# One layer's x + layernorm(x): from an addition on GpSimd to a second activation on ScalarE

## The chip, the core and the metric

The kernel runs on one core of a Trainium2 chip. A core has five engines that work side by side and meet at semaphores: TensorE (PE, matmuls and their weight loads), VectorE (DVE), ScalarE (ACT), GpSimd (POOL, which also starts transfers from its own queue) and SyncE (SP, which only starts transfers). The metric is the device time of one execution in microseconds; the time before is the median of three runs, 3288.75 us (3285.65 to 3289.74).

## The reference, cut to what matters

Four layers over x of 4 batches, 1024 rows, 256 columns, all float32:

```
x = x + attention_a(layernorm(x))    # 16 heads of 64
x = x + ffn(layernorm(x))            # 256 -> 1024, gelu, -> 256
x = x + attention_b(layernorm(x))    # layer 3: its function takes h = layernorm(x)
x = x + ffn(layernorm(x))
```

Attention b is called with h = layernorm(x). It normalizes h again (with a scale and a bias), projects down to two 128-wide codes, up to queries, keys and values, rotates queries and keys, and returns out + h: its own residual is the normalized input. So layer 3 is x + h + (the projected attention). The first two terms, x + layernorm(x), are what this case is about. With mean m and r = 1/sqrt(var + eps), layernorm(x) is x * r + (-m * r), and the sum is x * (1 + r) + (-m * r).

## The kernel before, in words

All of x stays on chip, one tile per batch (`xs[b]`, 128 partitions x 8 row tiles x 256 columns), and is updated in place by every layer. The order of work on each engine is written out by hand: the kernel runs under a manual schedule, and each engine executes its instructions in the order in which the Python code issues them.

An attention layer is a sequence of 256 steps: 4 batches x 8 pairs of heads x 8 query tiles of 128 rows (`steps_with`, from line 330). In a step TensorE makes the scores of the next query tile (`scores`, L238) into one of three score buffers for each of the two heads; VectorE takes the negated row maximum (L249); ScalarE makes the exponentials with their row sums (`exponentials`, L251); VectorE inverts the sums (L259), ScalarE spreads them over columns beside the exponentials (`invert`, L260), and VectorE transposes blocks of 32 x 32 into the tile T (`turn`, L271). Every second step, transfers rearrange T into pT: the last five of each group start from GpSimd's queue, the others from SP's (`send`, L295). TensorE multiplies pT by the values (`weigh`, L304) five steps behind; ScalarE copies the sums out (L314) and, in the second attention, copies one block of T to pT itself (`keep`, L287); GpSimd multiplies by the inverted row sums (`take`, L316); TensorE projects (`project`, L167), ScalarE copies the result out (L326) and GpSimd adds it to x (L328).

Work for the following pair and batch is hung into the steps through a table of pieces: the function `batch_b` gives each of its pieces a step number, and `steps_with` runs them after the exponentials or at the end of that step. The projections of the next pair (L647, L668 on ScalarE), the exchange of neighbouring rows (L652, transfers from GpSimd's queue) and the rotation (L657 to L659, three GpSimd operations) are such pieces. The weights of a pair come over SP's queue (L636, L212, L214).

`batch_b` prepares a batch for attention b in two blocks of four row tiles (qb = 0 and 1, t = 0 to 3). Its piece `first` makes layernorm(x) of one row tile into x1 with a ScalarE activation (`standardize`, L147) and lets GpSimd add it to x (L604). `second`, two steps later, scales x1 in place on ScalarE for the second normalization (L608), and `turned` transposes it on TensorE and copies it out (L153, L158). Batches 1 to 3 are prepared within the steps of the batch before them, one tile per step; batch 0 is prepared within the feed-forward layer ahead, where `rest` takes one or two pieces of this prologue behind each GELU (L414) of the last blocks.

The factors of a normalization are measured and finished by `scaling`: statistics (L126, L127) on VectorE, a square root on ScalarE (L130), and the reciprocal and products on VectorE (L131 to L138). In layer 3 it runs three times, over 8, 16 and 8 row tiles.

In the feed-forward layer (`ffn`) a block of 512 rows is standardized on ScalarE (L147, four activations in a row) with GpSimd adding the second bias to x (L396), transposed on TensorE and copied out by ScalarE (L156), multiplied into three buffers in turn (L410), passed through the GELU (L414), multiplied back (L421) and added to x on VectorE (L428).

Of the kernel before, what the change touches and what calls it, by code (L numbers as in the profile page):

```python
# [9 lines left out]
F32 = mybir.dt.float32  # L10
# [5 lines left out]
P = 128  # L16
# [7 lines left out]
NQB = S // QB  # L24
# [15 lines left out]
def hybrid_block_kernel(  # L40
# [5 lines left out]
    nc = tc.nc  # L46
# [3 lines left out]
    const = ctx.enter_context(tc.tile_pool(name="const", bufs=1))  # L50
# [8 lines left out]
    def group(*shape):  # L59
        last[0] ^= 1  # L60
        return ps_mm.tile([P, *shape], F32, tag=f"m{last[0]}", name="mm")
# [45 lines left out]
    def scaling(name, blocks, again=False):  # L107

        where = {}
        for b, qb in blocks:
            for t in range(TQ):
                where[b, qb * TQ + t] = len(where)
        m = len(where)
        mv = const.tile([P, m, 2], F32, name=f"{name}_mv")
        rstd = const.tile([P, m], F32, name=f"{name}_rstd")  # L120
        shift = const.tile([P, m], F32, name=f"{name}_shift")
        more = const.tile([P, m], F32, name=f"{name}_more") if again else None

        def measure(b, t):
            stats = small.tile([P, 6], F32, tag="stats", name="stats")
            nc.vector.bn_stats(stats, xs[b][:, t, :])  # L126
            nc.vector.bn_aggr(mv[:, where[b, t], :], stats)  # L127

        def finish():
            nc.scalar.activation(rstd, mv[:, :, 1], AF.Sqrt, bias=eps)  # L130
            nc.vector.reciprocal(rstd, rstd)  # L131
            if again:
                nc.vector.tensor_mul(more, mv[:, :, 1], rstd)
                nc.vector.tensor_mul(more, more, rstd)
                nc.scalar.activation(more, more, AF.Sqrt, bias=eps)
                nc.vector.reciprocal(more, more)
            nc.vector.tensor_mul(shift, mv[:, :, 0], rstd)
            nc.vector.tensor_scalar_mul(shift, shift, -1.0)  # L138

        def get(b, t):  # L140
            i = slice(where[b, t], where[b, t] + 1)
            return shift[:, i], rstd[:, i], more[:, i] if again else None

        return measure, finish, {k: (lambda k=k: get(*k)) for k in where}

    def standardize(dst, src, shift, rstd):
        nc.scalar.activation(dst, src, AF.Identity, scale=rstd, bias=shift)  # L147

    def transposed(dst, src, c, affine=None):

        tr = group(TQ, P)
        for t in range(TQ):
            nc.tensor.transpose(tr[:, t, :], src[:, t, ts(c, P)], ident)  # L153
        trf = tr.rearrange("p t q -> p (t q)")
        if affine is None:
            nc.scalar.copy(dst[:, c, :], trf)  # L156
        else:
            nc.scalar.activation(  # L158
                dst[:, c, :], trf, AF.Identity,
                scale=affine[0][:, c : c + 1], bias=affine[1][:, c : c + 1],  # L160
            )

    def paired(out, parts, first=True, last=True):

        for i, (lhsT, rhs) in enumerate(parts):
            for j in range(2):
                nc.tensor.matmul(  # L167
                    out[ts(j, DH)], lhsT[:, ts(j, DH)], rhs[j],
                    start=(first and i == 0), stop=(last and i == len(parts) - 1),
                )  # L170
# [413 lines left out]
    def layer_b(rows):  # L584

        scale_b = 1.0 / 8.0
        cs = {}

        def batch_b(b):
            work = []  # L590
            for qb in range(NQB):
                k = {}

                def first(t, b=b, k=k, qb=qb):
                    if t == 0:
                        if b:
                            k["x1"] = xnp.tile([P, TQ, D], F32, tag="xn", name="x1")
                        else:
                            k["x1"] = ptp.tile([P, SENT], F32, tag="pT", name="x1")[
                                :, : TQ * D  # L600
                            ].rearrange("p (t d) -> p t d", t=TQ)
                    xt = xs[b][:, qb * TQ + t, :]
                    standardize(k["x1"][:, t, :], xt, *rows.factors(NQB * b + qb, t)[:2])
                    nc.gpsimd.tensor_add(xt, xt, k["x1"][:, t, :])  # L604

                def second(t, b=b, k=k, qb=qb):
                    x1 = k["x1"][:, t, :]
                    nc.scalar.mul(x1, x1, rows.factors(NQB * b + qb, t)[2])  # L608

                def turned(c, b=b, k=k, qb=qb):  # L610
                    if c == 0:
                        p, tag = (highp, f"high{qb}") if b % 2 == 0 else (lowp, "low")
                        cs[b, qb] = p.tile([P, NC, QB], F32, tag=tag, name="hc")
                    transposed(cs[b, qb], k["x1"], c, affine=(lns_sb, lnb_sb))

                def down(m, b=b, qb=qb):

                    h = cs[b, qb][:, :, ts(m, QB // 2)]
                    pc = group(2, QB // 2)
                    for i in range(2):  # L620
                        paired(pc[:, i], [(wd_sb[:, i, c, :], [h[:, c]] * 2) for c in range(NC)])
                    nc.scalar.copy(h, pc)

                work += [(16 * qb - 14 + t, lambda t=t, f=first: f(t)) for t in range(TQ)]
                work += [(16 * qb - 12 + t, lambda t=t, f=second: f(t)) for t in range(TQ)]
                work += [(16 * qb - 8 + 2 * c - EARLY, lambda c=c, f=turned: f(c)) for c in range(NC)]
                work += [(16 * qb + 2 * m, lambda m=m, f=down: f(m)) for m in range(2)]
            return work

        def pair_b(b, pr):  # L630
            made, turned = {}, {}

            def load():
                w = made["w"] = wp.tile([P, 3, NC, P], F32, tag="w", name="w")[:, :, 0, :]
                for i, up in enumerate((wuq, wuk, wuv)):
                    nc.sync.dma_start(w[:, i], up[:, ts(pr, P)])  # L636

            def qk(i, qb):

                pq = group(QB)  # L640
                paired(pq, [(made["w"][:, i, :], [cs[b, qb][:, i]] * 2)])
                name = ("qT", "kT")[i]
                if qb == 0:
                    made[name] = qkp.tile([P, S], F32, tag=name, name=name)
                straight = made[name][:, ts(qb, QB)]
                made[i, qb] = straight
                nc.scalar.mul(straight, pq, (scale_b, 1.0)[i])  # L647

            def change(i, qb):
                turned[i, qb] = rp.tile([P, QB], F32, tag="turned", name="turned")  # L650
                for r in range(2):
                    nc.gpsimd.dma_start(turned[i, qb][r::2], made[i, qb][1 - r :: 2])  # L652

            def rotate(i, qb):

                straight, other = made[i, qb], turned.pop((i, qb))
                nc.gpsimd.tensor_mul(straight, straight, cos_sb[:, ts(qb, QB)])  # L657
                nc.gpsimd.tensor_mul(other, other, sin_sb[:, ts(qb, QB)])
                nc.gpsimd.tensor_add(straight, straight, other)  # L659

            def values(qb):
                if qb == 0:
                    made["v"] = vp.tile([P, NK2, DH], F32, tag="v", name="v")
                pv = group(NK2 // NQB, DH)
                for t in range(NK2 // NQB):
                    lhsT = cs[b, qb][:, 1, ts(t, DH)]
                    by_head(pv[:, t, :], [(lhsT, made["w"][:, 2, :])])
                nc.scalar.copy(made["v"][:, ts(qb, NK2 // NQB), :], pv)  # L668

            work = []  # L670
            for i in (1, 0):
                for qb in range(NQB):
                    k = 2 - 4 * i + 2 * qb
                    work += [(k - EARLY, lambda i=i, qb=qb: qk(i, qb))]
                    work += [(k + 1, lambda i=i, qb=qb: change(i, qb))]
                    work += [(k + 2, lambda i=i, qb=qb: rotate(i, qb))]
            work += [(4 + 2 * qb - EARLY, lambda qb=qb: values(qb)) for qb in range(NQB)]
            return {name: lambda name=name: made[name] for name in ("qT", "kT", "v")}, load, work

        return attention(batch_b, pair_b, wo_b, nc.sync, lead=5, kept=1)  # L680
# [8 lines left out]
    end_b, rest_b, _ = ffn_between(Rows("g", sets), True, n_steps)  # L689
# [66 lines left out]
```

## Time and profile before

| | before |
|---|---|
| median of three runs | 3288.75 us (3285.65, 3288.75, 3289.74) |
| profiled execution | 3283.29 us, its span 3281.4 us |
| mean granted TensorE clock | 0.996 |
| first attention, feed-forward, second attention, feed-forward | to about 1421, 1676, 3023, 3281 us of the span |
| GpSimd's additions L604 | 32, 734 ns (median), from 1562.9 to 2572.7 us |
| ScalarE's activations L147 of layer 3 | 32, 597 ns (median), from 1562.1 to 2571.1 us |

The profile is a record of one execution. It gives for every engine its busy time, for groups of equal instructions their count, their mean duration and what ended the idle time before them, and it follows the chain of waits back from the last instruction. L-numbers are lines of the kernel before. A timeline row has the start, the duration, the engine, the line, the operation, output and inputs, the count of instructions merged into the row, and in brackets the idle time before it with what released it. A row of a chain has the start, the time, the engine, what it worked on and the line. In a row of stretches the columns are the stretch and its length, then busy time and instruction count of TensorE, its weight loads, VectorE, ScalarE and GpSimd, the granted clock, the busy share of the DMA engines and what they moved in GB/s. The ends of matmuls are modelled, so that the end of one can lie a little past the start of the next.

### The profile page before, as it was taken

How to read it: one execution, taken by the hardware profiler on the slowest of the kernel's cores; microseconds unless marked ns; L12 is line 12 of the kernel's file. 1: busy time of each engine (PE TensorE's matmuls, PEld its weight loads, DVE VectorE, ACT ScalarE, POOL GpSimd, SP SyncE). 2: the span in 40 equal slices, each digit the busy share in tenths (PEclk: the TensorE clock that was granted, in tenths of full speed). 3: DMA queues.
4: the chain of work that ended last, by engine and by line, in shares of the span. 5: the costliest groups of instructions: out<-in, count | busy, mean ns of one | idle time of the engine just before them, and what ended most of it. 6: DMA issues, size and time to landing. Idle time of an engine off the chain costs nothing.

```text
span 3281.4 us, 126564 instructions
## 1 busy us (share of the span) xinstructions
PE 3201.6 (98%) x52736; PEld 2022.3 (62%) x52736; DVE 2531.3 (77%) x2386; ACT 2109.0 (64%) x4304; POOL 1958.4 (60%) x2738
## 2 busy tenths in 40 slices
PE   8999999999999999999999999999999999998999
PEld 4666666666666666666555556666656666665666
DVE  7988888888888888941049889998989999998100
ACT  5666666666666666642447777777778777777332
POOL 4544454545444445430159888998989999996110
PEclk9999999999999999999999999999999999999999
DMA  8888888888888888840029889998888899998100
GB/s 226 224 220 213 226 223 222 219 227 223 222 214 218 222 229 225 218 116 0 2 81 237 223 217 240 242 240 236 240 229 240 240 243 247 245 246 214 38 20 20
DMA packets 244697, 642.13 MB, mean 196 GB/s; under 512 B 74304, under 2 KB 102976, under 8 KB 244128
## 3 DMA queue, kind: packets, MB, share of 16 engines
q1 hardware_dynamic: 161104, 397.60, 47.6%
q0 software_dynamic: 83024, 236.44, 25.8%
q8 instruction: 419, 6.86, 0.9%
q14 instruction: 150, 1.23, 0.1%
HBM read 43.39 MB, written 4.19 MB: 15 GB/s over the span
## 4 chain that ended last, share of the span: by engine, by line
PE 78%; SPq 8%; DMA 5%; DVE 3%; ACT 3%; issue 3%; POOL 1%; DVEq 0%; POOLq 0%; ACTq 0%
PE sc L238 23%; PE mm L304 21%; PE mm L167 16%; SPq L295 7%; PE mm L421 7%; PE ph L410 7%; PE mm L176 5%; DMA pT<-T 4%; DVE T L271 1%; DVE nmax L249 1%; ACT p L251 1%; PE mm L153 1%; POOL oT L316 0%; ACT gT L414 0%; SPq L214 0%
## 5 line engine op out<-in xcount | busy, mean ns | idle before, releaser
L249 DVE TENSOR_REDUCE nmax<-sc 128x1 f32<-128x1024 f32 x1024 | 1204.5, 1218 | 226.7 <-PE sc L238 223.5
L251 ACT ACTIVATE p<-sc,nmax 128x1024 f32<-128x1024 f32 x1024 | 1145.3, 1119 | 324.0 <-DVE nmax L249 324.0
L271 DVE STREAM_TRANSPOSE T<-p 128x2176 f32<-128x2176 f32 x512 | 1247.1, 2436 | 41.0 <-DMA pT<-T 17.6
L238 PE MATMUL sc<-kT,qT 64*64 64x512 f32 x8192 | 1085.5, 599 | 16.0 <-ACT p L251 10.6
L304 PEld LDWEIGHTS mm<-pT,v 64*64 64x64 f32 x32768 | 950.3, 133 | 145.6 <-issue 103.4
L304 PE MATMUL mm<-pT,v 64*64 64x128 f32 x32768 | 984.5, 269 | 14.5 <-issue 13.5
L295 POOL DMA_DIRECT2D pT<-T x1280 | 629.6, 499 | 121.1 <-PE sc L238 56.2
L316 POOL TENSOR_TENSOR oT<-oT,pT 128x256 f32<-128x256 f32 x256 | 186.1, 727 | 718.7 <-ACT oT L314 636.3
L238 PEld LDWEIGHTS sc<-kT,qT 64*64 64x64 f32 x8192 | 333.1, 133 | 409.9 <-issue 277.1
L328 POOL TENSOR_TENSOR x<-x,got 128x512 f32<-128x512 f32 x256 | 330.9, 1293 | 27.8 <-ACT got L326 23.9
L326 ACT COPY got<-mm 128x512 f32<-128x512 f32 x256 | 150.0, 586 | 283.0 <-PE mm L167 282.9
L428 DVE TENSOR_TENSOR x<-x,mm 128x512 f32<-128x512 f32 x32 | 22.0, 687 | 367.2 <-PE mm L421 367.1
L167 PE MATMUL mm<-wo,oT 128*64 128x256 f32 x2048 | 278.4, 393 | 19.6 <-POOL oT L316 18.6
L167 PEld LDWEIGHTS mm<-wo,oT 128*64 128x64 f32 x2048 | 124.6, 136 | 266.4 <-POOL oT L316 217.4
L414 ACT ACTIVATE gT<-ph,b_sb 128x512 f32<-128x512 f32 x128 | 87.5, 686 | 301.9 <-PE ph L410 301.8
L260 ACT COPY p<-total 128x128 f32<-128x128 f32 x512 | 151.8, 296 | 195.4 <-DVE total L259 188.5
L167 PE MATMUL mm<-hT,w 128*64 128x512 f32 x1024 | 242.9, 596 | 1.0 <-ACT hT L156 1.0
L421 PE MATMUL mm<-w_sb,gT 128*128 128x256 f32 x1024 | 226.0, 381 | 6.6 <-ACT hT L156 6.6
L410 PE MATMUL ph<-hT,w_sb 128*128 128x512 f32 x512 | 230.2, 603 | 0.5 <-ACT hT L156 0.5
L421 PEld LDWEIGHTS mm<-w_sb,gT 128*128 128x128 f32 x1024 | 193.1, 190 | 39.4 <-ACT hT L156 9.4
L396 POOL TENSOR_TENSOR x<-x,b_sb 128x256 f32<-128x256 f32 x64 | 44.5, 728 | 275.6 <-ACT xn L147 275.6
L251 ACT ACTIVATION_READ_ACCUMULATOR p<-sc,nmax 128x1 f32 x1024 | 205.3, 200 | 0.0
(90 smaller groups left out, 2473.1 us busy)
## 6 DMA issues: line engine op xcount, KB each, us to landing
pT<-T SPq DMA_DIRECT2D x2688, 136.0 KB, 4.7
pT<-T POOLq DMA_DIRECT2D x1280, 136.0 KB, 4.7
turned<-kT POOLq DMA_DIRECT2D x128, 128.0 KB, 3.5
turned<-qT POOLq DMA_DIRECT2D x128, 128.0 KB, 3.3
w<-in_wqkv_a POOLq DMA_DIRECT2D x96, 128.0 KB, 6.1
wo<-in_wo_a POOLq DMA_DIRECT2D x32, 128.0 KB, 5.4
wo<-in_wo_a POOLq DMA_DIRECT2D x64, 64.0 KB, 5.5
wo<-in_wo_b SPq DMA_DIRECT2D x32, 128.0 KB, 3.6
```

The lines of the kernel that those rows point to most:

```text
L167: nc.tensor.matmul(out[ts(j, DH)], lhsT[:, ts(j, DH)], rhs[j], start=(first and i == 0), stop=(last and i == len(parts) - 1),)
L176: nc.tensor.matmul(out[ts(j, DH)], lhsT, rhs[:, ts(j, DH)], start=(i == 0), stop=(i == len(parts) - 1),)
L238: nc.tensor.matmul(sc[s, j][ts(half, DH), ts(m, 512)], qT()[rows, ts(2 * qs + half, DH)], kT()[rows, ts(m, 512)], start=True, stop=True,)
L249: nc.vector.tensor_reduce(nmax, sc[s, j], AX.X, ALU.max, negate=True)
L251: nc.scalar.activation(probs[s][:, :NK2, ts(j, 2), :], sc.pop((s, j)).rearrange("p (k c i) -> p k c i", c=2, i=SQ), AF.Exp, bias=nmax, acc ...
L271: nc.vector.transpose(T[h][:, :, q, :, :].rearrange("p c k i -> p k c i"), probs.pop(s))
L295: engine.dma_start(pT[h][ts(c, SQ), a], T[h][ts(a, SQ), c])
L304: nc.tensor.matmul(av[h][q][ts(j ^ q, DH)], v[ts(j, DH), k, :], pT[h][ts(j, DH), :, q, k, :], start=(k == 0), stop=(k == NK2 - 1),)
L316: nc.gpsimd.tensor_mul(parts, parts, pT.pop(h)[:, :, :, NK2, :])
L328: nc.gpsimd.tensor_add(xd, xd, got)
L410: nc.tensor.matmul(ph, w1_sb[:, c, ts(f, P)], hT[n][:, c, :], start=(c == 0), stop=(c == NC - 1),)
L421: nc.tensor.matmul(po[n][:, t % 2, :], gT[n][:, f, ts(t, P)], w2_sb[:, f, :], start=(f == 0), stop=(f == NF - 1),)
```

## The change

In layer 3, `scaling` also makes plus = r + 1, one more VectorE operation behind the others in each of its three calls. `first` calls `standardize` a second time, from x to x itself, with the scale plus and the same bias, and GpSimd's addition goes. Behind every L147 of layer 3, ScalarE's order gets one activation of the same shape; VectorE's order gets three small instructions; GpSimd's loses 32; TensorE's and SP's are the same as before. In the instruction order of the changed program each new activation waits for ScalarE's own completion count, since it overwrites what the activation ahead of it reads; the other activations of layer 3's preparation do not have this wait.

```diff
         more = const.tile([P, m], F32, name=f"{name}_more") if again else None
+        plus = const.tile([P, m], F32, name=f"{name}_plus") if again else None
...
             nc.vector.tensor_mul(shift, mv[:, :, 0], rstd)
             nc.vector.tensor_scalar_mul(shift, shift, -1.0)
+            if again:
+                nc.vector.tensor_scalar_add(plus, rstd, 1.0)
...
-            return shift[:, i], rstd[:, i], more[:, i] if again else None
+            return (shift[:, i], rstd[:, i]) + ((more[:, i], plus[:, i]) if again else ())
...
                     xt = xs[b][:, qb * TQ + t, :]
-                    standardize(k["x1"][:, t, :], xt, *rows.factors(NQB * b + qb, t)[:2])
-                    nc.gpsimd.tensor_add(xt, xt, k["x1"][:, t, :])
+                    shift, rstd, _, plus = rows.factors(NQB * b + qb, t)
+                    standardize(k["x1"][:, t, :], xt, shift, rstd)
+                    standardize(xt, xt, shift, plus)
```

## The prediction

> **What bounds the kernel now.** I read the page first, for the bound of the whole and the chain that ended last; then the groups by shape, for the two operations that the change trades; then the timelines of ScalarE, GpSimd and TensorE in the eight places where these run.
>
> ```profile
> span 3281.4 us, 126564 instructions
> ...
> PE 3201.6 (98%) x52736; PEld 2022.3 (62%) x52736; DVE 2531.3 (77%) x2386; ACT 2109.0 (64%) x4304; POOL 1958.4 (60%) x2738
> ...
> POOL 4544454545444445430159888998989999996110
> ...
> PE 78%; SPq 8%; DMA 5%; DVE 3%; ACT 3%; issue 3%; POOL 1%; DVEq 0%; POOLq 0%; ACTq 0%
> ```
>
> TensorE is busy 98% of the span and makes 78% of the last chain. GpSimd is at 60% on average, but at 8 or 9 tenths in slices 22 to 36, the second attention layer, where most of the removed additions stand. The groups:
>
> ```profile
> L604 POOL TENSOR_TENSOR x<-x,x 128x256 f32<-128x256 f32 x32 | 23.4, 733 | 32.2 <-DVE b_mv L127 16.8 <-ACT x L147 15.0
> ...
> L147 ACT ACTIVATE x<-x,b_shift,b_rstd 128x256 f32<-128x256 f32 x32 | 19.3, 605 | 0.0
> ```
>
> So 32 additions of 733 ns leave GpSimd (23.4 us), and 32 activations of the second row's kind come to ScalarE. Both are under 1% of the span; what counts is who waits. Eight of each lie in the feed-forward layer before (batch 0, 1562 to 1625 us), 24 in attention: six blocks of four tiles, t0 to t3, from about 1787, 1877, 2133, 2217, 2471 and 2555 us, one tile per step of about 5.2 us.
>
> The chain of waits inside the fifth block is TensorE without a gap, and ScalarE's timeline there shows how near it is:
>
> ```profile
> 2486.34 1.72 PE sc L238 x16
> 2488.05 1.01 PE mm L167 x8
> ...
> 2490.88 1.97 PE sc L238 x16
> ```
>
> ```profile
> 2482.78 0.62 ACT L147 ACTIVATE x<-x,b_shift,b_rstd 128x256 f32<-128x256 f32 x1
> 2483.28 0.53 ACT L608 ACTIVATE x<-x,b_more 128x256 f32<-128x256 f32 x1
> 2483.68 0.31 ACT L260 COPY p<-total 128x128 f32<-128x128 f32 x1
> 2484.29 1.11 ACT L251 ACTIVATE p<-sc,nmax 128x1024 f32<-128x1024 f32 x1 [0.30 <-DVE nmax L249]
> ...
> 2487.94 0.59 ACT L147 ACTIVATE x<-x,b_shift,b_rstd 128x256 f32<-128x256 f32 x1
> 2488.44 0.49 ACT L608 ACTIVATE x<-x,b_more 128x256 f32<-128x256 f32 x1
> 2488.84 0.28 ACT L260 COPY p<-total 128x128 f32<-128x128 f32 x1
> 2489.17 0.59 ACT L326 COPY got<-mm 128x512 f32<-128x512 f32 x1
> 2489.65 1.12 ACT L251 ACTIVATE p<-sc,nmax 128x1024 f32<-128x1024 f32 x1
> ```
>
> In t2's step (2482.78) ScalarE has 0.30 us to spare before the first exponential; in t3's (2487.94) nothing is waited for up to the exponential at 2489.65. That one ends at 2490.77, and TensorE's scores at 2490.82 need its score buffer (three in turn, two used per step). So t3's ScalarE work stands 0.1 us from the bound.
>
> **The cost of one new activation.** Four activations of L147 in a row take 2.06 us (1624.89): 0.59 and three times 0.49, so they overlap by 0.1. The Trainium skill ("ScalarE: Activation LUTs", section "What ACT_TABLE_LOAD costs") says the same of back-to-back ACTIVATEs, about 93 ns; by it one more costs 0.49. But the new one writes xt, which the one before it reads, and in the changed program it waits for ScalarE's own completion. No row shows this wait on ScalarE at work; the nearest are VectorE's dependent pairs, which start 0.04 us after the end (L133 at 1679.38 for 0.17, L134 at 1679.59). I take 0.59 + 0.04 before it starts instead of 0.49, so 0.14 more: 0.63 us per new activation. Bounds: 0.49 if the wait is free, 0.73 if it costs as much again as the overlap. All 32 together: 20 us at 0.63, by the rule 15.7.
>
> **In the attention blocks (24).** Behind the new activation on ScalarE wait L608 (t2, t3), the copy of 1/total (L260), the copy of the projection (L326) and the exponentials (L251). t0: 0.8 us or more of waiting for L249 follows, which hides it. t1: L326 waits for TensorE by 1.42, 0.44, 0.38, 0.44, 1.60 and 0.45 us in the six blocks; over that stick out 0, 0.19, 0.25, 0.19, 0, 0.18, and L259 was already waiting for the exponential (0.15 at least), so it carries on. t2: 0.53 in the first block, 0.30 in the others: 0.10, then 0.33 each. t3: 0.63 each, less L326's wait, 0, 4.3, 0.73, 0.48, 0 and 0.57. Added up per block: 0.73; hidden; 0.48; 0.67; 0.96; 0.57. Together 3.4 us (at 0.49: 1.6).
>
> Is a late exponential dearer than its own lateness? Once the trace shows what a hold-up grows to: GpSimd's send at 1887.81 came 2.87 us late and its step (1894.3 to 1904.2) took 9.92 us where its neighbours took 5.17, so 4.75 more, 1.65 times. I take that factor, since VectorE, TensorE and the transfers (DMA share 0.88 in these blocks) are all near full there: 3.4 x 1.65 = 5.6 us. Without it 3.4; with all hidden, 0.
>
> **In the feed-forward layer (8).** TensorE is the bound here too (246.65 busy of 256 us from 1420). Four of the eight (1562 to 1567) come one per GELU, each GELU 1.72 us apart on TensorE, and 0.58 from a GELU to the next start, 0.63 and 0.49 make 1.70: nothing. One at 1603.91 is followed by 0.54 of waiting: nothing that matters. The other three stick out:
>
> ```profile
> 1605.63 0.59 ACT L147 ACTIVATE x<-x,b_shift,b_rstd 128x256 f32<-128x256 f32 x1
> 1606.12 1.06 ACT L156 COPY hT<-mm 128x512 f32<-128x512 f32 x2
> ```
>
> The copies L156 start when ScalarE is free, and TensorE's L421 waits for them (0.87 at 1606.75): 0.63 more. At 1623.17 two stand together; with nothing waited for up to the L608s, TensorE's transposes behind them already wait (0.64 at 1628.77): 1.26. Sum 1.9 us.
>
> **What GpSimd's relief brings.** The rule that speaks for the change is in "GPSIMD Engine Reference" (section "Engine selection"): elementwise work with two inputs does not belong on GpSimd. By that alone 23.4 us of a nearly full engine would come back. The trace agrees on the price but not on the worth: TensorE waits for L316 with L604 right ahead of it in only four places, 0.62, 0.36, 0.46 us and this one:
>
> ```profile
> 1895.34 0.72 POOL L604 TENSOR_TENSOR x<-x,x 128x256 f32<-128x256 f32 x1
> 1896.02 0.72 POOL L316 TENSOR_TENSOR oT<-oT,pT 128x256 f32<-128x256 f32 x1
> ```
>
> ```profile
> 1896.79 1.98 PE L167 MATMUL mm<-wo,oT 128*64 128x256 f32 x8 [3.30 <-POOL oT L316]
> ```
>
> The three small ones are in the sum already, as L326's slack of t3. The fourth gives 0.7 us. The sends (L295) behind the second addition of a pair move up by up to 0.74 us; their stall was a queue's wait, not L604, so I give them nothing. VectorE's three new instructions of 8 or 16 columns are 0.17 us each like L138, 0 to 0.5 us in all; two stand right ahead of work that others wait for (1680.5 and 1855.1): I take 0.3. L328's additions into x come many steps later: nothing.
>
> **Sum.** 5.6 + 1.9 - 0.7 + 0.3 = about +7.1 us. The profiled execution took 3283.29 us (its span and 1.9 around it), so 3290.4 for its like. It is 5.46 below the median of the three runs, 3288.75; on that, 3295.8 us, +0.22%.
>
> **The rivals.** (1) Slower by far: ScalarE becomes the bound of the blocks. If t0 and t1 lose their slack too, because VectorE and TensorE start earlier once GpSimd is relieved, 24 x 0.63 = 15.1 and 1.9 give +17, 3306; half of that 3297. It decides from about 0.8 us exposed per block on average (6.6 less 1.9, by six). For it: t3 has no slack in two blocks. Against: t0 waits 0.82 for L249, and that is VectorE's own length. (2) Absorbed: the delay falls into later stalls for transfers, as at 1961.96 (TensorE 1.71 us) or 2133.05 (VectorE 1.98 us for pT). Then only the feed-forward's 1.9 us and what lies before no stall remain: +2, 3290.7. (3) GpSimd's relief wins. In the hold-up of 1894 the granted clock falls to half:
>
> ```profile
> 1898.00:1902.00 4.00, 4.00 (x40) 2.18 (x36) 0.24 (x1) 2.24 (x4) 3.98 (x7) 0.50 0.99 269
> ```
>
> The matmuls of L167 take 1.98 instead of 1.08 us. The skill ("TensorE: Matmul & The Clock Gate", Part 1) lets the clock fall after an idle window of 3.4 us; the wait was 3.30 and the clock did fall, so the sizes agree, and 0.7 us less of waiting could keep it. At half speed for 6.8 us that is 3.4 us. With 0.7, and 3 us of sends that start earlier, -7, less what sticks out in the feed-forward, and ScalarE hidden: -5 to -8, about 3282. It needs the drop to recur in every execution, which one trace can't show. (4) The change does not do what it says: no wait, overlap kept, 0.49 each: 1.6 x 1.65 + 1.5 - 0.7 = +3.4, 3292.
>
> **How the numbers follow.** A measurement of this kernel can tell about 0.2%, 6.6 us, from no change: 3282.2 to 3295.3. The likeliest case, exposed at t2 and t3, has 50%, its own range 3292 to 3300; I put 36 of it beyond 0.2% and 14 within. Rival 1 has 14%, all slower. Rivals 2 and 4 together 24%, within. Rival 3 has 12%, 9 faster and 3 within. So slower 0.50, same 0.41, faster 0.09. The range leaves out the far half of rival 1 and most of rival 3: 3285 to 3303.
>
> **What would show it.** Right: the new group has 32 entries of about 0.6 us on ScalarE, its start 0.6 and more after L147's; L326 and L251 in t3 follow ScalarE and not TensorE or VectorE; "PE sc <- ACT p" and L259's wait for L251 grow; L421 near 1607 waits 0.6 longer. Wrong: new and old activation 0.5 apart; blocks that take as long as before; a clock that stays full near 1896 with that step under 6 us (rival 3); t0's exponential waiting for no VectorE (rival 1).

## The result, and the profile after

| | before | after |
|---|---|---|
| median | 3285.74 us (3280.79 to 3293.35, 14 runs) | 3295.73 us (3286.74 to 3301.99, 14 runs) |
| ratio | | 1.0026, 95% interval 1.0017 to 1.0035 |
| profiled execution | 3283.29 us | 3293.02 us |

The kernel is slower by 0.26%, about 8.5 us (5.6 to 11.5). The forecast was +7.1 us and 3295.8. That the number was met says little for its working: the experiments below show that two of its terms were wrong and that a third, larger than either, was not in it. Even the agreement of 3295.8 with 3295.73 is in part chance, since the kernel before came out 3.0 us lower over 14 runs than over the three that the forecast started from.

In the changed kernel everything behind the added lines stands a few lines lower: L147 is L150, L249 to L328 are three further, L421 is L424, L608 is L612. The page of after:

```profile
span 3291.2 us, 126568 instructions
...
PE 3211.0 (98%) x52736; PEld 2021.5 (61%) x52736; DVE 2531.0 (77%) x2389; ACT 2122.2 (64%) x4336; POOL 1937.3 (59%) x2706
...
POOL 4544454545454445430158799888888888986110
...
PE 65%; SPq 17%; DMA 6%; ACT 5%; DVE 3%; issue 3%; POOL 1%; ACTq 0%; DVEq 0%
```

GpSimd lost its 32 additions (2738 to 2706 instructions, 21 us), ScalarE gained 32 activations. In the last chain TensorE's share falls from 78 to 65% and SP's queue, which issues transfers, rises from 8 to 17%. Most of that rise is scatter of single profiles: in six further kernels without the slower transfers described below, SP's queue has 12 to 14%. The two groups of layer 3, old and new:

```profile
L150 ACT ACTIVATE x<-x,b_shift,b_rstd 128x256 f32<-128x256 f32 x32 | 19.3, 604 | 0.0
L150 ACT ACTIVATE x<-x,b_shift,b_plus 128x256 f32<-128x256 f32 x32 | 19.2, 601 | 1.1
```

ScalarE's timeline at t3 of the fifth attention block, then TensorE's row behind it, before and after:

```profile
2490.20 0.60 ACT L150 ACTIVATE x<-x,b_shift,b_rstd 128x256 f32<-128x256 f32 x1
2490.83 0.60 ACT L150 ACTIVATE x<-x,b_shift,b_plus 128x256 f32<-128x256 f32 x1
2491.34 0.49 ACT L612 ACTIVATE x<-x,b_more 128x256 f32<-128x256 f32 x1
2491.74 0.28 ACT L263 COPY p<-total 128x128 f32<-128x128 f32 x1
2491.92 0.57 ACT L329 COPY got<-mm 128x512 f32<-128x512 f32 x1
2492.40 1.11 ACT L254 ACTIVATE p<-sc,nmax 128x1024 f32<-128x1024 f32 x1
```

```profile
2489.83 1.06 PE L167 MATMUL mm<-hc,w 128*64 128x512 f32 x4
...
2492.55 1.08 PE L170 MATMUL mm<-hc,w 128*64 128x512 f32 x4 [0.36 <-ACT got L329]
```

The new activation starts 0.63 us after the old one, 0.03 after its end, where independent activations overlap by 0.1 (2490.83 to 2491.34). TensorE now waits 0.36 us for L329, where it did not wait before. In the feed-forward layer (TensorE's row again before and after):

```profile
1609.56 0.60 ACT L150 ACTIVATE x<-x,b_shift,b_plus 128x256 f32<-128x256 f32 x1
1610.06 1.05 ACT L159 COPY hT<-mm 128x512 f32<-128x512 f32 x2
```

```profile
1606.75 14.08 PE L421 MATMUL mm<-w_sb,gT 128*128 128x256 f32 x64 [0.87 <-ACT hT L156]
...
1610.68 2.64 PE L424 MATMUL mm<-w_sb,gT 128*128 128x256 f32 x11 [1.49 <-ACT hT L159]
```

TensorE's wait grew from 0.87 to 1.49, by the 0.62 that was forecast. So far all as foreseen. Two things are not. The hold-up of the second block, which cost half a clock before, is shorter:

```profile
1894.00:1898.00 4.00, 4.00 (x112) 2.89 (x104) 4.00 (x4) 4.00 (x10) 3.92 (x4) 1.00 1.01 278
1898.00:1902.00 4.00, 2.68 (x48) 1.73 (x44) 3.46 (x4) 3.24 (x7) 4.00 (x7) 1.00 0.52 128
```

The granted clock is 1.00 throughout. The step that took 9.92 us takes 5.03, and the ten steps around it 53.8 us instead of 58.2. That is a gain of about 4 us, yet the execution is 10 us longer. And the transfers take longer. Their two queues and the group of VectorE's transposes into T (last part: its idle time and what ended most of it) on the page of before, then of after:

```profile
q1 hardware_dynamic: 161104, 397.60, 47.6%
q0 software_dynamic: 83024, 236.44, 25.8%
...
L271 DVE STREAM_TRANSPOSE T<-p 128x2176 f32<-128x2176 f32 x512 | 1247.1, 2436 | 41.0 <-DMA pT<-T 17.6
```

```profile
q1 hardware_dynamic: 161104, 397.60, 48.2%
q0 software_dynamic: 83024, 236.44, 26.0%
...
L274 DVE STREAM_TRANSPOSE T<-p 128x2176 f32<-128x2176 f32 x512 | 1247.5, 2437 | 70.2 <-DMA pT<-T 42.9
```

Packets and bytes are the same and the span is longer, so the larger shares mean slower packets. VectorE waits 29 us more before its transposes, most of it for transfers that still read the T tile it wants to overwrite. In the packet records a 4352-byte packet of pT<-T on q1 takes 271 ns in the median where it took 265, and the 4096-byte packets on q0, among them the exchanges turned<-kT and turned<-qT, 180 ns where they took 166.

### The profile page after: what moved, and what is told of

It reads as the page before. It is cut to its first block, busy times and chain, and to the rows that moved or that the text cites. A ratio compares the mean times of both kernels' runs of the same rounds, so it can differ in the third digit from the quotient of the medians.

```text
span 3291.2 us, 126568 instructions
## 1 busy us (share of the span) xinstructions
PE 3211.0 (98%) x52736; PEld 2021.5 (61%) x52736; DVE 2531.0 (77%) x2389; ACT 2122.2 (64%) x4336; POOL 1937.3 (59%) x2706
## 4 chain that ended last, share of the span: by engine, by line
PE 65%; SPq 17%; DMA 6%; ACT 5%; DVE 3%; issue 3%; POOL 1%; ACTq 0%; DVEq 0%
PE sc L241 18%; PE mm L307 17%; SPq L298 16%; PE mm L170 13%; PE mm L424 7%; PE ph L413 6%; DMA pT<-T 5%; PE mm L179 4%; ACT p L254 2%; DVE T L274 1%; DVE nmax L252 1%; SPq L217 1%; POOL oT L319 1%; PE mm L156 1%; ACT gT L417 1%
## 5 line engine op out<-in xcount | busy, mean ns | idle before, releaser
L274 DVE STREAM_TRANSPOSE T<-p 128x2176 f32<-128x2176 f32 x512 | 1247.5, 2437 | 70.2 <-DMA pT<-T 42.9
L329 ACT COPY got<-mm 128x512 f32<-128x512 f32 x256 | 149.7, 585 | 278.0 <-PE mm L170 278.0
L424 PE MATMUL mm<-w_sb,gT 128*128 128x256 f32 x1024 | 226.0, 381 | 7.2 <-ACT hT L159 7.2
L413 PE MATMUL ph<-hT,w_sb 128*128 128x512 f32 x512 | 229.1, 600 | 0.0
L424 PEld LDWEIGHTS mm<-w_sb,gT 128*128 128x128 f32 x1024 | 193.1, 190 | 40.0 <-ACT hT L159 10.0
```

What stands on the lines that cost most here:

```text
L274: nc.vector.transpose(T[h][:, :, q, :, :].rearrange("p c k i -> p k c i"), probs.pop(s))
L413: nc.tensor.matmul(ph, w1_sb[:, c, ts(f, P)], hT[n][:, c, :], start=(c == 0), stop=(c == NC - 1),)
L424: nc.tensor.matmul(po[n][:, t % 2, :], gT[n][:, f, ts(t, P)], w2_sb[:, f, :], start=(f == 0), stop=(f == NF - 1),)
```

## The experiments

Every ratio is to the kernel before, with its 95% interval; 0.1% is 3.3 us. Each kernel ran 10 to 22 times.

**1. The change in parts.** The plus tile with its three VectorE instructions, without the trade:

```diff
+        plus = const.tile([P, m], F32, name=f"{name}_plus") if again else None
...
+            if again:
+                nc.vector.tensor_scalar_add(plus, rstd, 1.0)
...
                     standardize(k["x1"][:, t, :], xt, shift, rstd)
                     nc.gpsimd.tensor_add(xt, xt, k["x1"][:, t, :])
```

> GpSimd's additions stay, and only the tile plus and its three VectorE instructions are added. Theory 1 (ScalarE's late exponentials cost the time): -1 to +1 us against before. Rival 2 (the time comes from what the new tile does aside from ScalarE: every tile behind it is allocated a little further on, and in the profiled execution after the change the first attention layer, whose instructions are the same, already ended 4.5 us later, 1426.5 instead of 1422.0 us): +4 us or more, and the first attention again ends at 1425 us or later.

Measured: 3292.4 us, 1.0021 (1.0013 to 1.0029), +6.9 us. Nearly the whole slowdown stands without a single new ScalarE activation. The other sign that rival 2 named, a later end of the first attention, did not come: the last transpose of the first attention starts at 1422.2 us here (1422.4 before, 1426.8 in the profile of after).

The additions left out, nothing put in:

```diff
                     standardize(k["x1"][:, t, :], xt, *rows.factors(NQB * b + qb, t)[:2])
-                    nc.gpsimd.tensor_add(xt, xt, k["x1"][:, t, :])
```

> GpSimd's 32 additions are left out with nothing in their place, so layer 3 leaves its own input out of the sum: GpSimd's relief alone. Theory 1: it gains little, 0.7 us (the one addition ahead of the late L316) to 2 us, so -2 to 0 us. Rival 3 (the relief wins by itself, ScalarE eats it up): -5 us or more. Rival 4 (an earlier GpSimd queue starts transfers into others and costs): +3 us or more.

Measured: 3282.0 us, 0.9991 (0.9983 to 1.0): GpSimd's relief is worth some 3 us (0 to 5.6) where 0.7 was forecast.

The plus tile and the new activations, beside the additions:

```diff
+        spare = const.tile([P, D], F32, name="spare")
...
                     standardize(k["x1"][:, t, :], xt, shift, rstd)
+                    standardize(spare, k["x1"][:, t, :], shift, plus)
                     nc.gpsimd.tensor_add(xt, xt, k["x1"][:, t, :])
```

> The additions stay on GpSimd and ScalarE gets the 32 new activations all the same, at the same place and with the same wait for its own completion, but they read x1 and write a spare tile that nothing reads: ScalarE's cost alone. Theory 1: +7 to +10 us, that is the whole of the change and the 0.7 to 2 us of relief on top. Rival 3: +10 to +15 us. Rival 2: no more than the kernel with the tile alone.

Measured: 3295.19 us, 1.003 (1.0021 to 1.004): the activations add 0.09% to the plus tile's 0.21%.

The whole change once more:

> The changed kernel once more, beside the others, for a second trace of it. All theories: +6 to +11 us. Theory 1: the feed-forward layer's transposes and GELUs of 1600 to 1640 us are 1.7 us later by the same three activations; the blocks at t0 to t3 repeat their step lengths within 0.1 us where no transfer is late. Rival 2: the first attention ends 4 us later than before again.

Measured: 3291.24 us, 1.0017 (1.0009 to 1.0025). The slowdown is 5.6 us here and 8.5 us above; the intervals overlap. In this trace, too, the first attention does not end 4 us later (1423.3 us).

**2. What does a tile cost that only holds factors?** All four kernels have the same stream of transfers, but the three with the plus tile have slower packets (271, 272 and 269 ns on q1; 264 without it). The three plus tiles take 32, 64 and 32 bytes of each partition, ahead of all working buffers. In the built program before, T begins at byte 97,792 of a partition (191 x 512), pT at 132,608 (259 x 512), and they and all the working buffers behind them start on multiples of 512. With the plus tiles all of these start 128 bytes over one (1152 bytes further on where the spare tile came as well). So I moved the buffers and changed no instruction:

```diff
+        pad = 32 if name == "g2" else 0
-        shift = const.tile([P, m], F32, name=f"{name}_shift")
+        shift = const.tile([P, m + pad], F32, name=f"{name}_shift")[:, :m]
```

> The kernel before with no instruction changed: the tile g2_shift is 128 bytes a partition longer, so that every tile of the later pools (T, pT, qk, x1's places and the rest) begins 128 bytes further on, as it does with the three new plus tiles; T's and pT's addresses are then 128 over a multiple of 512 where they were a multiple of it. Theory A (the addresses slow the transfers): the 4352-byte packets of the pT<-T transfers take 266 ns in the median instead of 261, the 4096-byte ones 180 to 187 instead of 166, and the time is 5 to 9 us over before (ratio about 1.002), as with the plus tile alone. Rival B (it was the three VectorE instructions, or a time that differs by build): packets at 261 and 166 ns and the time within 2 us of before.

Measured: 3291.51 us, 1.002 (1.0011 to 1.003). With the unchanged instructions of before, 128 unused bytes cost 6.6 us. The page of this kernel, in the same three rows:

```profile
q1 hardware_dynamic: 161104, 397.60, 48.4%
q0 software_dynamic: 83024, 236.44, 26.1%
...
L272 DVE STREAM_TRANSPOSE T<-p 128x2176 f32<-128x2176 f32 x512 | 1247.2, 2436 | 69.4 <-DMA pT<-T 30.5
```

They resemble after's rows: 69.4 us of idle time before the transposes against 70.2, larger shares on both queues. (Of the 69.4, transfers end 30.5, of after's 70.2 they end 42.9.) The packets take 271 and 187 ns. The engines that write the moved tiles show nothing of it: ScalarE is busy for 2107.1 us (2109.0 before) and VectorE for 2530.3 (2531.3).

The same with `pad = 128` and with `pad = 64` (512 and 256 bytes):

> The kernel before with no instruction changed: g2_shift is 512 bytes a partition longer, so the later tiles keep their place against multiples of 512 bytes. Theory A, in the form that alignment to 512 bytes decides: packets at 261 and 166 ns, time within 2 us of before. In another form (any move of the tiles slows them, or the distance to what lies before decides): as with 128 bytes, 266 ns and 5 to 9 us over. Rival B: within 2 us of before, with packets as before; it is then told apart by the 128-byte run.

> The kernel before with no instruction changed and g2_shift 256 bytes a partition longer. The blocks that pT<-T moves are 4352 bytes long and lie 4352 bytes apart, so already before every other one begins 256 over a multiple of 512. Theory A1 (being on a multiple of 256 decides): as before, 265 ns for the q1 packets of 4352 bytes and 166 ns for those of 4096, time within 2 us of before. Theory A2 (multiples of 512 decide, by the tile's own start): slower than before by some or all of the 7 us, with the 4096-byte packets, which start with their tile, at 175 ns or more.

Measured: 3283.79 us, 1.0001 (0.9992 to 1.001), and 3283.08 us, 1.0003 (0.9992 to 1.0013). The packets take 262 and 165 ns, and 264 and 165 ns. Both kernels are as before, so it is neither that tiles move nor that one of them grew. Of the expected forms the one with multiples of 256 holds; moves other than 128, 256 and 512 bytes (and 1024 and 1152 by way of other runs) were not tried.

**3. The change with the buffers in line.** The change and the plus tile alone, each with `pad = 96`, so that the shift is 512 bytes in all:

> The whole change, with g2_shift 384 bytes a partition longer, so that the later tiles lie 512 bytes further on than before and not 128. Theory A: what is left is ScalarE's added 0.63 us at 32 places against GpSimd's 32 additions less; without the additions the kernel ran 2.8 us under before, and ScalarE's copies beside the additions cost 2.8 us over the plus tile alone, so the two cancel and the time is within 3 us of before (3282 to 3288 where before runs 3285), with packets at 261 and 166 ns. Rival (the prediction's own sum, 7 us of ScalarE's exposures and nothing of the addresses): 5 to 9 us over before whatever the addresses.

> The plus tile and its three VectorE instructions alone, GpSimd's additions kept, with g2_shift 384 bytes a partition longer, so that the later tiles lie 512 bytes further on than before. Theory A: within 2 us of before, packets at 261 and 166 ns; the 7 us that the plus tile cost by itself are gone. Rival B (the VectorE instructions, or a tile more in the program): 5 to 9 us over before, as without the padding.

Measured: the change 3283.2 us, 1.0001 (0.999 to 1.0011); the plus tile with its VectorE instructions 3281.96 us, 0.9995 (0.9986 to 1.0005). The page of the change in line:

```profile
q1 hardware_dynamic: 161104, 397.60, 47.7%
q0 software_dynamic: 83024, 236.44, 25.8%
...
L275 DVE STREAM_TRANSPOSE T<-p 128x2176 f32<-128x2176 f32 x512 | 1247.2, 2436 | 40.0 <-DMA pT<-T 16.1
```

The trade of ScalarE for GpSimd itself makes no difference that can be told, and the transposes wait 40 us as they did before. The 4352-byte packets on q1 take 266 and 265 ns in these two kernels, as before; the 4096-byte ones take 173 and 171, a little more than the 165 to 168 of the other kernels in line, which no run explains. The 0.63 us of each new activation is still there in all 32 places.

**4. Which buffers?** The pad moved to the front of oT, which lies behind pT, so that only what follows moves by 128 bytes; then the reverse (32 more columns ahead as in the first pad, 96 in oT):

```diff
-            oT[h] = otp.tile([P, HB, P], F32, tag="oT", name="oT")
+            oT[h] = otp.tile([P, 32 + HB * P], F32, tag="oT", name="oT")[:, 32:].rearrange("p (q a) -> p q a", q=HB)
```

> The kernel before with no instruction changed; the tile oT is 128 bytes a partition longer at its front, so that p, T and pT stay on multiples of 512 bytes and everything behind them (qk, turned, x1's place, w, wo, v) begins 128 bytes over one. If the pT<-T transfers bring the loss: time within 2 us of before, q1's 4352-byte packets at 265 ns, only the 4096-byte ones (turned<-kT, turned<-qT) slower, 180 to 187 ns. If the others do: 4 to 7 us over before.

> The reverse: p, T and pT (and oT) begin 128 bytes over a multiple of 512, everything behind them on one; no instruction changed. If the pT<-T transfers bring the loss: 5 to 8 us over before, q1's 4352-byte packets at 271 ns, the 4096-byte ones at 166. If the others do: within 2 us of before.

Measured: the rest moved 3284.95 us, 1.0004 (0.9995 to 1.0013); p, T, pT and oT moved 3288.66 us, 1.0017 (1.0007 to 1.0026). The queues' rows, of the first and then of the second:

```profile
q1 hardware_dynamic: 161104, 397.60, 47.7%
q0 software_dynamic: 83024, 236.44, 26.0%
```

```profile
q1 hardware_dynamic: 161104, 397.60, 48.1%
q0 software_dynamic: 83024, 236.44, 25.6%
```

Each move slows the transfers of its own buffers and no others. With the rest moved, q0's 4096-byte packets take 181 ns (166) and q1's 4352-byte ones 265 (265); with T moved, 165 and 269. The move of p, T, pT and oT costs 5.6 us (2.3 to 8.5), and of these four only T and pT take part in transfers. The rest's 1.3 us (-1.6 to 4.3) can't be told from nothing. Together they make 6.9, near the 6.6 of the full move.

How the slower packets turn into time is not shown in full. VectorE's idle time before its transposes is 38.9 to 49.1 us in the seven profiles with the buffers in line (on multiples of 256) and 62.5 to 71.5 in the five with everything moved, but 49.1 with the rest moved and only 51.7 with T moved, although that kernel is slower. Nor is the place settled. The profiles point to the second attention (from its first to its last transpose 1344 to 1350 us in four kernels in line, 1349 and 1353 in two with everything moved) and not to the first (1390 to 1392, and 1391 and 1393), but one profile of each can't decide it.

**5. ScalarE's activations alone.** No plus tile and no VectorE instruction; the spare tile of 1024 bytes keeps the buffers on multiples of 512:

```diff
+        spare = const.tile([P, D], F32, name="spare")
...
+                    standardize(spare, k["x1"][:, t, :], shift, rstd)
                     nc.gpsimd.tensor_add(xt, xt, k["x1"][:, t, :])
```

> The kernel before with the 32 further ScalarE activations alone, each reading the x1 tile that the activation before it wrote and writing a spare tile of 1024 bytes a partition; GpSimd's additions are kept, there is no plus tile and no VectorE instruction, and the later tiles lie 1024 bytes further on, on multiples of 512 as before. Theory A with ScalarE's cost as the plus-tile runs gave it: 2 to 4 us over before (ratio 1.0006 to 1.0012), packets as before. Rival (the prediction's sum without its relief): 7.5 us over. Rival (ScalarE's time is hidden): within 1 us.

Measured: 3286.46 us, 1.0011 (1.0002 to 1.002), +3.6 us (0.7 to 6.6): inside the 2 to 4 us that theory A gave, and half of the 7.5 us of the prediction's sum, which lies just outside the interval.

**Put together.** Every kernel is a choice of three: buffers in line or 128 bytes off, additions kept or gone, new activations or none. Ratios:

| | additions, none new | additions and new | no additions, none new | no additions, new |
|---|---|---|---|---|
| in line | 1; 1.0001; 1.0003; 0.9995 | 1.0011 | 0.9991 | 1.0001 |
| 128 bytes off | 1.002; 1.0021 | 1.003 | not run | 1.0017; 1.0026 |

Down a column, the 128 bytes cost 0.16 to 0.26% wherever they come. The activations cost 0.11 and 0.10% in line and 0.09% off it, and the missing additions give 0.09 and 0.10% in line, 0.13 and 0.04% off it. Each single figure is uncertain by about 0.1%, and the pairs share kernels, so they are fewer separate checks than they look; but none contradicts another. The three add up: 6.6 + 3.6 - 3.0 = 7.2 us, where the change measured 8.5 and 5.6. No kernel that does the same work came out under the one before by more than its interval.

## Why the prediction was right in its total and wrong in its working

The total was luck. The attention blocks were put some 3.7 us too high and GpSimd's relief 2.3 too low, which makes 6.0 us too many, and 6.6 us from the buffers' addresses were left out.

**The activation's cost: right.** The new activations start 0.63 us after the old ones in the median of the 32 (0.62 to 0.67), in each of the five profiles that have them. Rival (4), the rule's 0.49, falls: the wait on ScalarE's own completion takes the overlap away.

**The feed-forward layer, 1.9 us: right.** The wait near 1607 grew by 0.62, and the stage from the first L413 of the last block but one to its fifth from 9.10 to 10.21 us, 1.11 against 1.26. The whole stretch from the L413 beside the first new activation to the first L413 of the last block takes 96.0 us in the nine profiles without new activations and 97.7 in four of the five with them: 1.7 us. In the fifth, the second trace of the change, it takes 99.4; there the clock fell to half for 3.4 us at 1631.6.

**The attention blocks, 5.6 us: too large, in both of its parts.** The first part, the 3.4 us of lateness, was mis-sized. After the change, t2 of the fifth block reads:

```profile
2484.96 0.63 ACT L150 ACTIVATE x<-x,b_shift,b_rstd 128x256 f32<-128x256 f32 x1
...
2486.71 1.10 ACT L254 ACTIVATE p<-sc,nmax 128x1024 f32<-128x1024 f32 x1
```

From the old activation to the exponential behind it are 1.75 us, where the rows before have 1.51 (2482.78 to 2484.29): 0.24 late, not 0.33. At t1 it is mostly 1.80 instead of 1.71, 0.09 late, and at t3 of the fifth block 2.20 instead of 1.71, 0.49 late and not 0.63. Added up as the prediction did, over the five blocks other than the second, this gives 2.4 us with the buffers in line.

The second part is "I take that factor": a hold-up of 2.87 us that also halved the clock was made the rule for delays of a tenth to a half of a microsecond. No run supports it. Of ScalarE's 3.6 us in all, the feed-forward layer takes 1.7, so 1.9 are left for the 24 places, less than the 2.4 without any factor; with the interval (-1.0 to 4.9) the 5.6 us are excluded, and a factor on the 2.4 is not. In the five blocks other than the second, the 50 steps with activations take 263.4 and 262.7 us with the buffers in line, and 262.1, 264.0, 264.8 and 260.7 us without: no lengthening beyond the scatter of some 2 us. So rival (2), that the blocks' delay is absorbed later and about +2 us remain, is not excluded either. Rival (1) is: at t0 the exponential still waits 0.4 us or more for VectorE.

**GpSimd's relief, 0.7 us: too small.** Rival (3)'s mechanism is what happens, at its one place: a late L316 behind an addition, and a clock that falls. Its signs came too, a full clock there and that step under 6 us (5.0 to 5.9 in the four profiles without additions). The prediction gave the moved sends nothing and the hold-up of 1894 only the addition's 0.7 us. In all ten profiled kernels that keep the additions, the longest step of the second block takes 7.2 to 9.9 us; in all four that lack them, 5.9 to 6.1. The stretches of that place with the plus tile in line (additions kept), then without additions:

```profile
1892.00:1896.00 4.00, 0.71 (x10) 0.07 (x4) 3.03 (x5) 1.71 (x4) 3.92 (x5) 0.87 0.28 84
1896.00:1900.00 4.00, 4.00 (x42) 2.88 (x44) 2.14 (x1) 1.99 (x4) 3.98 (x8) 0.50 0.73 212
```

```profile
1892.00:1896.00 4.00, 2.71 (x44) 1.74 (x44) 4.00 (x3) 2.46 (x6) 4.00 (x8) 1.00 0.45 123
1896.00:1900.00 4.00, 4.00 (x95) 3.14 (x97) 2.34 (x4) 3.21 (x9) 3.99 (x5) 1.00 1.00 262
```

GpSimd is full in both. With the additions TensorE does 0.71 us of work in the first stretch and then runs at half its clock; without them the gap is shorter and the clock stays full. The drop came here in eight of the ten and in none of the four, so it does recur, which the prediction left open. The ten steps around it are 57.2 us on average with the additions and 53.8 without: 3.4 us, as much as the whole of the relief measured. Of rival (3) the price failed: it had 5 to 8 us net (its own terms give about 5), and ScalarE's cost takes back what the relief gives.

**VectorE's instructions, 0.3 us: not to be seen.** With the buffers in line they measured -1.6 us (-4.6 to 1.6).

**What was not in the sum: the addresses, 6.6 us (3.6 to 9.9).** The prediction costed the tile plus by the three instructions that fill it and never asked where the buffers behind it come to lie. None of the rivals had it. It is the largest term, and it alone makes the change slower; without it the change would have been a draw.

**Small slips of the working.** The third block's own entries (0.25 and 0.33) make 0.58 where its sum has 0.48, and the 1.6 us at 0.49 come to nearly 2 from the same waits. The row at 1961.96, which rival (2) takes for a wait for transfers, has "issue" as its end: TensorE waited there for nothing that the profile shows. None of these changes the account.

## What to carry to other kernels

A new tile moves every tile that is allocated after it: before a small slowdown is put down to the instructions of an edit, run the old instructions with the same padding, or the edit padded back to the old alignment. Look for it in rows that the edit does not touch: the queues' share at the same packets and bytes, and waits for transfers. A trade between engines is best measured as a table, each part with and without the other: here three terms of 0.1 to 0.2% that no single profile could separate added up in every cell, within the noise.

## What the runs showed of the hardware that was not expected

- Packets between tiles in on-chip memory take longer where the tiles start 128 bytes over a multiple of 256. On q1, 4352 bytes take 262 to 266 ns in the seven profiles in line (one of them 256 over a multiple of 512) and 269 to 272 in the five with everything moved by 128; 4096 bytes on q0 take 165 to 173 and 180 to 187. Shifts by 256, 512 and 1024 bytes cost no time beyond the noise. The 4352-byte packets on q0 hardly differ (251 and 252 ns); why is open, and no run here shows what in the memory or the transfer engines causes the rest.
- With the 128 unused bytes the packets fill 42 us more of each transfer engine (2409 to 2451 us on q1 and q0 together, one profile each), of which 6.6 us appear in the time.
- A 128x256 activation that must wait for the one ahead of it on ScalarE starts 0.63 us after that one's start, where an independent one starts after 0.49 to 0.50.
